# A four-layer graph network on one core: how layer 2's masks are applied, when they are made, and the order of TensorE's work

## The chip, the core and the metric

The kernel runs on one core of a Trainium2 chip. The core has five engines that matter here. TensorE (PE) multiplies matrices, with the loading of its stationary operand shown apart (PEld). VectorE (DVE) does elementwise work and reductions, ScalarE (ACT) functions of one argument and copies, GpSimd (POOL) a few powers. SyncE (SP) issues the transfers. Every engine works through its own queue in order and waits on semaphores for the others. The metric is the device time of one execution, in microseconds; less is better.

## The reference, cut to what matters

There are 32 graphs of 512 nodes with 256 features, and an adjacency matrix of 512 x 512 for each. Four attention layers follow each other, each with a residual and a layer norm around it:

```python
x = _layernorm(x + L0(x, adj))   # 4 heads; scores from two vectors, masked by adj, softmax, sum
x = _layernorm(x + L1(x, adj))   # 1 head, the same kind, elu
x = _layernorm(x + L2(x, adj))   # a transformer block, 8 heads, feed forward of 1024
x = _layernorm(x + L3(x, adj))   # 1 head, the same kind as layer 1
```

Layer 2 is the one that the change is about:

```python
allowed = (adj > 0) | (swapaxes(adj, 1, 2) > 0) | eye
scores = einsum('bhqd,bhkd->bhqk', q * scale, k)
scores = where(allowed[:, None], scores, -inf)
attn = softmax(scores, axis=-1)
ctx = einsum('bhqk,bhkd->bhqd', attn, v)
```

Layers 0, 1 and 3 use adj itself; layer 2 uses its symmetric closure with the diagonal.

## The kernel before

**Tiling.** A graph's 512 nodes lie in R = 4 blocks of 128 rows; the features in K = 2 blocks of 128. Each layer is written as a Python generator that yields ahead of each unit of TensorE's work. A unit is one block of rows of a projection, one block of columns of a transpose, one pair of score tiles, or one weighted sum.

**The order.** `graph(b)` (L711) strings the stages of graph b together, and `paced` (L101) gives every unit a key: `PERIOD * b` plus a number from the table `PLACES` (L31). `heapq.merge` (L729) runs the units of all graphs in the order of the keys. So work of three to four graphs is interleaved, and TensorE's order is exactly the order in which the units run (`manual_schedule` for that engine, L728). The order on the other engines is chosen by the scheduler of the language, and is fixed in the built program. Keys are only an order: they are no times.

**Stages and buffers.** The stages have buffer pools of their own: "a" for edges, layers 0 and 1, "b" for qkv, attention and projection, "c" for feed forward and layer 3. `bank` (L240) gives a PSUM bank: four for stage b, two each for a and c. `part` (L245) gives a tile of 128 x 512 from 8, 6 and 5 buffers. `project` (L311) makes a projection, with one buffer h in each stage.

**Edges and masks.** `load` (L340) loads adj transposed (adjt) and adj in two halves each, all four through one buffer. `masks` (L350) makes, on ScalarE, two passes over each half of adjt: a Copy into the byte mask `at` (3 buffers) and a Square, whose sums are compared later to verify that the entries are 0 or 1. Then VectorE takes the maximum with adj and with the identity on the diagonal. The first half becomes a byte mask a2m; the second half becomes a2a in bf16, turned into 0 or -2^127 (L370). All this stands at one place, `"edges"`, ahead of layer 0.

**Layers 0, 1, 3.** `along` (L328) lays a vector of a head along the free dimension with a transpose (gp) and a copy (gb). `kept` (L373) makes a tile of unnormalised attention in one VectorE step (L376): a maximum, times `at`. TensorE multiplies these tiles with the values (o; L403 in layer 0, L433 in layers 1 and 3). Layer 0 ends with a norm by head (`head_layernorm`, L275, with a power on GpSimd) and a layer norm (`layernorm`, L252, with another).

**Layer 2.** `qkv` (L468) makes q and k as sums of two parts (hi, lo), which 64 transfers a graph lay out in the tiles qk, and v. `attention` (L518) runs over four pairs of heads and four blocks j of keys. For each it makes two score tiles s (L527) and takes exp on ScalarE (L536). The mask comes in two ways: for j = 0 and 1 VectorE multiplies the exponentials of both heads with the byte mask (L539); for j = 2 and 3 TensorE adds 0 or -2^127 to the scores in PSUM, by a product of the identity with a2a (L535):

```python
if j in ADDED:
    nc.tensor.matmul(s, identb, a2[1][:, j % 2, :], start=False, stop=True)
nc.scalar.activation(t[:, i, :], s, AF.Exp, scale=QSCALE)
...
if j not in ADDED:
    edges = a2[0][:, j, :].unsqueeze(1).to_broadcast([P, 2, N])
    nc.vector.tensor_mul(t, t, edges)
```

Four such j are summed with v on TensorE (cp, L547) and copied (cs, L555). `attended` (L559) transposes cs, divides (L570, L574; ctx), transposes again (ctp) and projects (wop). `feed_forward` (L598) follows, with f1p, ft and f2p, and a residual and two norms; then `layer3` (L643).

**The engines' queues at these places.** SP issues the edge loads, x and xt, the qk layouts and the outputs, in one order. ScalarE's queue holds the Copy and Square passes between exps and evacuations; VectorE's holds the maxima between multiplications and norms.

## Time and profile before

| what | value |
|---|---|
| time, median of 3 runs (lowest, highest) | 3973.95 us (3971.76, 3975.07) |
| the profiled execution: its time, its span | 3970.98 us, 3969.2 us |
| granted TensorE clock, mean | 0.981 |
| L535, mask products on TensorE (385 of 512 on record) | 150.8 us busy, 392 ns listed |
| L539, multiplications by the mask on VectorE, x256 | 309.8 us busy, 1221 ns each |
| L536, exp on ScalarE, x1024 | 546.3 us busy, 605 ns listed |
| L361 and L364, Copy and Square passes | 1057 and 1041 to 1058 ns each |
| L366, maxima with adj | 1214 to 1216 ns each |
| ScalarE's wait at L361 for the load of adjt | 106.9 us, 32 times |
| ScalarE's wait at L361 for the mask buffer (DVE pt) | 20.0 us, 29 times |

How to read it: a row of the profile gives engine and line, operation, what it writes and reads, how often, and busy time with the mean of one. Consecutive instructions of one engine overlap at their ends, so the distance between two starts is the cost, and the listed duration is more than that. A wait names the instruction that ended it. Some records of products are missing from the trace.

### The profile page before, as it was taken

What the parts mean: (1) busy time and instruction counts of PE and PEld (TensorE: products, weight loads), DVE (VectorE), ACT (ScalarE), POOL (GpSimd) and SP (SyncE); (2) the same over time, 40 slices, a digit from 0 to 9 for tenths busy, and PEclk for the clock granted to TensorE, in tenths of its full rate; (3) what the DMA queues carried; (4) which work ended last, traced back from release to release, by engine and by line L of the source; (5) the groups of instructions that cost most, each with busy time, mean ns of one, the idle gap of its engine ahead of it and who ended that gap; (6) DMA issues with size and microseconds to landing.
All of it is one profiled execution on the core that took longest, in us unless ns stands there. A gap on an engine that the chain in (4) does not pass through costs nothing.

```text
span 3969.2 us, 53826 instructions
## 1 busy us (share of the span) xinstructions
PE 3806.5 (96%) x19367; PEld 2824.3 (71%) x19494; DVE 2523.9 (64%) x5402; ACT 1959.5 (49%) x4257; POOL 294.5 (7%) x266
## 2 busy tenths in 40 slices
PE   5899999999999999999999999999999999999996
PEld 4577767777767777777777777777777777777654
DVE  4557666667666667666667666667666667666543
ACT  2435555545555545555545555545455544555442
POOL 0000010000000000000000000000000000000000
PEclk6899999999999999999999999999999999999998
DMA  3222222222222222122222122222222222221110
GB/s 126 63 68 67 66 60 59 70 80 69 65 63 56 70 80 78 56 65 58 65 80 80 55 65 57 64 80 80 58 65 55 69 75 80 60 66 51 48 48 12
DMA packets 180432, 261.23 MB, mean 66 GB/s; under 512 B 36800, under 2 KB 72768, under 8 KB 180160
## 3 DMA queue, kind: packets, MB, share of 16 engines
q1 hardware_dynamic: 180160, 257.71, 23.3%
q8 instruction: 157, 2.57, 0.3%
q14 instruction: 115, 0.94, 0.1%
HBM read 106.57 MB, written 16.78 MB: 31 GB/s over the span
## 4 chain that ended last, share of the span: by engine, by line
PE 50%; DVE 17%; ACT 12%; issue 9%; POOL 5%; POOLq 0%; DVEq 0%; ACTq 0%
PE o L403 10%; ACT y L267 6%; PE f2p L627 6%; PE f1p L612 6%; PE o L433 6%; PE qkp L477 5%; POOL rs L262 3%; PE cp L547 3%; DVE pr L539 3%; PE h1p L318 3%; PE vp L504 3%; PE wop L588 3%; DVE bn L258 2%; POOL st L289 2%; PE gp L333 2%
## 5 line engine op out<-in xcount | busy, mean ns | idle before, releaser
L376 DVE SCALAR_TENSOR_TENSOR pt<-gb,ex,at 128x512 f32<-128x512 f32 x768 | 532.0, 745 | 359.2 <-ACT gb L337 358.4
L536 ACT ACTIVATE pr<-s 128x512 f32<-128x512 f32 x1024 | 546.3, 605 | 160.2 <-PE s L527 93.3
L267 ACT ACTIVATE y<-y,rs 128x256 f32<-128x256 f32 x768 | 398.5, 590 | 323.1 <-DVE rs L263 322.9
L403 PEld LDWEIGHTS o<-hv,pt 128*128 128x128 f32 x4096 | 506.4, 199 | 34.4 <-issue 20.2
L403 PE MATMUL o<-hv,pt 128*128 128x65 f32 x4096 | 503.3, 280 | 8.1 <-DVE pt L376 8.1
L433 PE MATMUL o<-h,pt 128*128 128x257 f32 x2048 | 488.2, 386 | 17.7 <-ACT exp L460 14.7
L627 PE MATMUL f2p<-wf,ft 128*128 128x256 f32 x2048 | 491.3, 383 | 10.6 <-ACT ft L621 5.3
L612 PE MATMUL f1p<-yt,wf 128*128 128x256 f32 x2048 | 488.7, 381 | 2.6 <-ACT yt L296 2.6
L547 PE MATMUL cp<-pr,v 128*64 128x512 f32 x2048 | 469.6, 600 | 3.7 <-DVE pr L539 3.7
L539 DVE TENSOR_TENSOR pr<-pr,a2m 128x1024 f32<-128x1024 f32 x256 | 309.8, 1221 | 253.2 <-ACT pr L536 253.1
L433 PEld LDWEIGHTS o<-h,pt 128*128 128x128 f32 x2048 | 375.7, 190 | 122.5 <-ACT exp L460 27.1
L527 PE MATMUL s<-qk 128*128 128x512 f32 x1024 | 450.4, 519 | 3.0 <-DMA qk<-lo 1.7
L627 PEld LDWEIGHTS f2p<-wf,ft 128*128 128x128 f32 x2048 | 379.2, 190 | 100.0 <-ACT ft L621 26.3
L612 PEld LDWEIGHTS f1p<-yt,wf 128*128 128x128 f32 x2048 | 384.7, 190 | 55.3 <-ACT yt L296 2.8
L621 ACT ACTIVATE ft<-f1p,cols 128x256 f32<-128x256 f32 x512 | 214.8, 471 | 401.6 <-PE f1p L612 401.6
L262 POOL TENSOR_TENSOR rs<-rs,mhalf 128x4 f32<-128x4 f32 x192 | 194.5, 1013 | 1904.7 <-DVE rs L261 1831.2
L547 PEld LDWEIGHTS cp<-pr,v 128*64 128x64 f32 x2048 | 136.0, 137 | 259.7 <-issue 229.5
L258 DVE BATCH_NORM_STATS2 bn<-y 128x6 f32<-128x256 f32 x768 | 297.3, 406 | 3.5
L337 ACT COPY gb<-gp 128x512 f32<-128x512 f32 x192 | 112.6, 586 | 338.3 <-PE gp L333 262.5
L477 PE MATMUL qkp<-xt,wqkv 128*128 128x512 f32 x512 | 236.5, 606 | 2.8 <-ACT xt L296 2.8
L527 PEld LDWEIGHTS s<-qk 128*128 128x128 f32 x1024 | 190.9, 194 | 57.9 <-issue 28.3
L411 DVE RECIPROCAL rd<-o 128x4 f32<-128x4 f32 x128 | 23.1, 181 | 270.9 <-PE o L403 270.9
(136 smaller groups left out, 4623.7 us busy)
## 6 DMA issues: line engine op xcount, KB each, us to landing
qk<-hi SPq DMA_DIRECT2D x1024, 64.0 KB, 2.0
qk<-lo SPq DMA_DIRECT2D x1024, 64.0 KB, 2.0
adjt<-in_adjt SPq DMA_DIRECT2D x64, 512.0 KB, 3.6
adj<-in_adj SPq DMA_DIRECT2D x64, 512.0 KB, 3.3
xt<-in_xt SPq DMA_DIRECT2D x32, 512.0 KB, 3.4
x<-in_x SPq DMA_DIRECT2D x32, 512.0 KB, 4.7
out<-y SPq DMA_DIRECT2D x32, 512.0 KB, 3.1
wf<-in_w1t SPq DMA_DIRECT2D x1, 1024.0 KB, 8.4
```

Of the source, the lines that this page charges most:

```text
L258: nc.vector.bn_stats(st[:, r, :], y[:, r, :])
L267: nc.scalar.activation(y[:, r, :], y[:, r, :], AF.Identity, bias=rs[:, 2, r : r + 1], scale=rs[:, 1, r : r + 1],)
L376: nc.vector.scalar_tensor_tensor(t, g, f, edges, op0=ALU.max, op1=ALU.mult)
L403: nc.tensor.matmul(o[:, r, :], pt[j][:, r * P : (r + 1) * P], hv[:, j, hh, :], start=j == 0, stop=j == R - 1,)
L433: nc.tensor.matmul(p[:, : D + 1], pt[j][:, r * P : (r + 1) * P], h[:, j, : D + 1], start=j == 0, stop=j == R - 1,)
L477: nc.tensor.matmul(p, wqkv[:, k, (s * K + c) * P : (s * K + c + 1) * P], xt[:, k, :], start=k == 0, stop=k == K - 1,)
L527: nc.tensor.matmul(s, qk[hp][:, 1, i, j * P : (j + 1) * P], qk[hp][:, 0, i, :], start=True, stop=j not in ADDED,)
L536: nc.scalar.activation(t[:, i, :], s, AF.Exp, scale=QSCALE)
L539: nc.vector.tensor_mul(t, t, edges)
L547: nc.tensor.matmul(cp[i * 2 * DH : (i + 1) * 2 * DH, :], v[:, j, first : first + 2 * DH], pr[j][:, i, :], start=j == 0, stop=j == R - 1,)
L612: nc.tensor.matmul(p[:, f, :], wf1[:, k, (ff + f) * P : (ff + f + 1) * P], yt[:, k, r * P : (r + 2) * P], start=k == 0, stop=k == K - 1,)
L627: nc.tensor.matmul(acc[:, i, :], ft[:, f, i * P : (i + 1) * P], wf2[:, ff + f, :], start=ff + f == 0 and i == 0, stop=ff + f == NF - 1 and ...
```

## The change

- `ADDED` and `SHUT` are gone: all 16 pairs of score tiles of a graph are multiplied by VectorE, and there is one byte mask a2 for all of adj's closure.
- The work on edges is split. `mask(b)` loads adjt half by half and makes `at` (now 4 buffers); the Square passes write into a `part` tile. `symmetric(b, at)` loads adj half by half and makes a2 (one buffer) in a stage of its own, `"mask"`, ahead of qkv.
- The first instruction of each such piece (the Copy, the maximum) is made to depend on the TensorE product that was issued last at its place (`product` records it, `in_place` adds the dependency). All products of the fast path are issued through `product`.
- `project` has two buffers h in stage a; `part` has seven in stage a for eight.
- Graph 0 loads xt and x ahead of its edges; xt's load stands ahead of the weights.
- All keys in `PLACES` are new.

```diff
-ADDED = (2, 3)
-SHUT = -(2.0**127)
 PERIOD = 1205
 PLACES = {
-    "edges": [-490],
-    "x": [-197],
+    "edges": [-226, -113, -5, -1],
+    "x": [84],
+    "mask": [1464, 1488, 1689, 1689],
     "layer 0": [
-        2, 11, 56, 83, 172, 302, 302, 302, 302, 302, 405, 405, 405, 405, 435, 533, 545, 545, 545,
-        553, 586, 586, 674, 674,
+        188, 232, 373, 373, 427, 532, 536, 536, 536, 549, 603, 603, 603, 630, 637, 712, 712, 728,
+        758, 758, 766, 779, 787, 791,
     ],
...
+    latest = [None]
+
+    def product(what, *args, **kwargs):
+        latest[0] = what(*args, **kwargs).ins.name
+
+    def in_place(op):
+
+        if latest[0]:
+            tc.add_manual_dep(op.ins, latest[0], ALL, reason="in its place")
+
...
-        return buf([P, N], "part", name, {"a": 8, "b": 6, "c": 5}[stage[0]])
+        return buf([P, N], "part", name, {"a": 7, "b": 6, "c": 5}[stage[0]])
...
-        h = buf([P, R, cols], "h", name, 1)
+        h = buf([P, R, cols], "h", name, {"a": 2}.get(stage[0], 1))
...
+    def half(b, name, h):
+        t = sb.tile([P, R // 2, N], I32, tag="adj", name=name, bufs=1)
+        rows = a[name][b, h * N // 2 : (h + 1) * N // 2]
+        nc.sync.dma_start(t, rows.rearrange("(r p) j -> p r j", p=P))
+        return t
+
+    def mask(b):
+
+        at = sb.tile([P, R, N], U8, tag="at", name="at", bufs=4)
         for h in range(2):
+            yield
+            t = half(b, "adjt", h)
             i = 2 * b + h
-            nc.scalar.activation(
-                at[:, half[h], :], adjt[h], AF.Copy, accum_out=sums[:, 0, i : i + 1]
-            )
-            nc.scalar.activation(a2[h], adjt[h], AF.Square, accum_out=sums[:, 1, i : i + 1])
+            yield
+            in_place(
+                nc.scalar.activation(
+                    at[:, h * R // 2 : (h + 1) * R // 2, :],
+                    t,
+                    AF.Copy,
+                    accum_out=sums[:, 0, i : i + 1],
+                )
+            )
+            squares = part("squares").bitcast(BF16).rearrange("p (r n) -> p r n", n=N)
+            nc.scalar.activation(squares, t, AF.Square, accum_out=sums[:, 1, i : i + 1])
+        return at
+
+    def symmetric(b, at):
+
+        a2 = sb.tile([P, R, N], U8, tag="a2", name="a2", bufs=1)
         for h in range(2):
-            nc.vector.tensor_max(a2[h], at[:, half[h], :], adj[h])
-        for r in range(R):
-            diag = a2[r * 2 // R][:, r % 2, r * P : (r + 1) * P]
-            nc.vector.tensor_max(diag, diag, identb)
-        nc.vector.tensor_scalar(a2[1], a2[1], 0.0, SHUT, op0=ALU.is_equal, op1=ALU.mult)
-        return at, a2
+            yield
+            t = half(b, "adj", h)
+            rows = slice(h * R // 2, (h + 1) * R // 2)
+            yield
+            in_place(nc.vector.tensor_max(a2[:, rows, :], at[:, rows, :], t))
+            for r in range(R // 2):
+                own = h * R // 2 + r
+                diag = a2[:, own, own * P : (own + 1) * P]
+                nc.vector.tensor_max(diag, diag, identb)
+        return a2
...
-                        stop=j not in ADDED,
+                        stop=True,
                     )
-                    if j in ADDED:
-                        nc.tensor.matmul(s, identb, a2[1][:, j % 2, :], start=False, stop=True)
                     nc.scalar.activation(t[:, i, :], s, AF.Exp, scale=QSCALE)
-                if j not in ADDED:
-                    edges = a2[0][:, j, :].unsqueeze(1).to_broadcast([P, 2, N])
-                    nc.vector.tensor_mul(t, t, edges)
+                edges = a2[:, j, :].unsqueeze(1).to_broadcast([P, 2, N])
+                nc.vector.tensor_mul(t, t, edges)
...
     def load_x(b):
         xt = sb.tile([P, K, N], F32, tag="xt0", name="xt0", bufs=1)
         nc.sync.dma_start(xt, a["xt"][b].rearrange("(k p) n -> p k n", p=P))
+        if b == 0:
+            weights0()
+        yield
         x = sb.tile([P, R, D], F32, tag="x", name="x")
         nc.sync.dma_start(x, a["x"][b].rearrange("(r p) d -> p r d", p=P))
-        yield
         return xt, x
...
-        at, a2 = yield from paced(b, "edges", load_all(b))
-        xt, x = yield from paced(b, "x", load_x(b))
+        if b == 0:
+            xt, x = yield from paced(b, "x", load_x(b))
+        at = yield from paced(b, "edges", mask(b))
+        if b:
+            xt, x = yield from paced(b, "x", load_x(b))
         x = yield from paced(b, "layer 0", layer0_all(b, x, xt, at, rds[0]))
         x = yield from paced(b, "layer 1", layer1_all(b, x, at, rds[1]))
+        a2 = yield from paced(b, "mask", symmetric(b, at))
         qk = yield from paced(b, "qkv", qkv_all(b, x))
```

What the new keys change in TensorE's order, read from the built programs: after the last layer-0 product of a graph the steps up to its layer-1 transposes are, in the new order, a feed-forward product f1p, two value projections, the scores of the first two pairs of heads of the graph before, with f2p, f1p, f2p, cp, f1p, f2p and cp between them. From the last f2p of the feed forward to layer 3's transposes come, in the old order, four score tiles with their masks, a layer-1 product, cp, three layer-1 products and the first steps of the next layer 0; in the new order two layer-1 products with two score tiles between them, cp, two more layer-1 products, and the transposes of the context and two layer-0 projections.

## The prediction

> **What bounds the kernel now.** I read the page's busy shares first, then the windows, to keep the ramps apart from the steady part, then the timeline of TensorE over some graphs, and last VectorE's timeline where attention runs. Busy shares and one wide window:

> ```profile
> span 3969.2 us, 53826 instructions
> PE 3806.5 (96%) x19367; PEld 2824.3 (71%) x19494; DVE 2523.9 (64%) x5402; ACT 1959.5 (49%) x4257; POOL 294.5 (7%) x266
> ...
> 200.00:3750.00 3550.00, 3491.87 (x18061) 2601.12 (x18181) 2336.50 (x5001) 1819.41 (x3959) 270.62 (x238) 1.00 0.24 67
> ```

> The window's columns are length, then busy time of TensorE, its weight loads, VectorE, ScalarE and GpSimd. TensorE works 98.4% of the middle. The other 105 us of its idle time lie in the first 200 and the last 220 us. The timeline shows one period, start of a graph's first layer-0 product to the next graph's:

> ```profile
> 1742.61 1.16 PE L318 MATMUL h0p<-w,xt 128*128 128x264 f32 x4 [0.34 <-ACT exp L460]
> 1861.21 1.16 PE L318 MATMUL h0p<-w,xt 128*128 128x264 f32 x4 [0.33 <-ACT exp L460]
> 1979.81 1.38 PE L318 MATMUL h0p<-w,xt 128*128 128x264 f32 x5 [0.34 <-ACT exp L460]
> ```

> The period is 118.60 us, the same each time: TensorE's order is fixed, and this is the sum of its steps and of a few waits that recur. What the mask costs there, and what a multiplication costs VectorE:

> ```profile
> 1803.60 1.04 PE L527 MATMUL s<-qk 128*128 128x512 f32 x2
> 1805.77 3.65 PE L547 MATMUL cp<-pr,v 128*64 128x512 f32 x16
> 1809.35 1.29 PE L527 MATMUL s<-qk 128*128 128x512 f32 x4
> 1810.48 1.89 PE L612 MATMUL f1p<-yt,wf 128*128 128x256 f32 x8
> ...
> 1813.23 1.23 DVE L290 TENSOR_TENSOR y<-y,st 128x1024 f32<-128x1024 f32 x1 [3.02 <-POOL st L289]
> 1814.37 1.22 DVE L539 TENSOR_TENSOR pr<-pr,a2m 128x1024 f32<-128x1024 f32 x1
> 1815.51 1.22 DVE L423 TENSOR_TENSOR y<-y,gam_b 128x1024 f32<-128x1024 f32 x1
> 1816.64 1.22 DVE L539 TENSOR_TENSOR pr<-pr,a2m 128x1024 f32<-128x1024 f32 x1
> ```

> Four scores with four added masks take 2.17 us (1803.60 to 1805.77), four without take 1.13 (1809.35 to 1810.48): a mask product costs 0.26 us of TensorE, whatever its listed 0.39. A multiplication costs VectorE 1.14 us, the distance between starts. VectorE also stands still for 3 us behind GpSimd's power (L289).

> [...]

> **The change, part by part.** Sums are per graph in the steady part, 118.60 us, and then over some 30 graphs, as the first and the last attention lie partly where TensorE idles anyway.

> *Removed.* 16 mask products of 0.26: 4.2 us of TensorE. On VectorE the L370 step, 0.4. The recurring stalls of the old order go too. In the period around 1861 TensorE's timeline shows 0.48 and 0.33 (layer 1's products and h0p, both behind ScalarE's exp L460) and 0.21 and 0.70 (h3p and gp, behind ScalarE). By strides it is more: three h3p projections take 3.96 us to the next gp (1867.99 to 1871.95) where three of 0.88 need 2.64, so 1.3 with the last two waits among it; layer 1's last three products take 0.9 too long, with the 0.48 among it; h0p 0.4 and some score pairs 0.4. I count 3.0. A stall-free period of the new order is then 118.6 - 4.2 - 3.0 = 111.4. Adding the new order's strides one by one gives 111.5.

> *Added to VectorE.* 8 multiplications a graph, 9.1 us: 256 x 1.14 = 292 us in all, less 13, so 2803 us or 71% of the span. On average that fits. It is the place that matters, so I walked one period of the changed order, engine by engine, with the durations of this trace (0.22 us from a product's end to its reader, 0.49 per exp in a row, 0.57 per copy of a bank, POOL 2.9 and 1.0). Three stretches:

> (a) From a graph's last layer-0 product to its layer-1 transposes TensorE has 23.2 us of steps, and the first two head pairs of the graph before fall there. VectorE must do layer 0's two norms (12 us), eight multiplications instead of four (9.1) and a feed-forward sum: 22 of 23.2. In the old kernel the stretch is 23.7 us with VectorE busy for 16.6. In the new order the fourth multiplication of the first head pair stands behind the step that waits for GpSimd's 2.9 us power; the weighted sum cp comes 0.4 late for it. ScalarE's Square of the next graph's edges (1.06 + 0.2) stands ahead of a feed-forward evacuation: 0.9. The second cp waits twice about 0.4 for its third and fourth multiplication, and the transposes 0.2 for ScalarE's normalisation. Together 2.0.

> (b) From there to layer 3: the sum that ends the feed forward now stands behind two multiplications and its norm behind a third, so that norm's end slips from 14.5 us after the last f2p product to about 17, while TensorE's steps up to layer 3's transposes shrink from 17.6 to about 15.4. On VectorE the context steps (L570, L574 of before) come after it. Layer 0's second projection waits 0.6 and the context's transposes 2.4 for these; layer 3's own transposes then find their data. Together 3.1.

> (c) The rest: 0.1 at gp, 0.45 for the fourth layer-0 tile of the third head. Together 0.6.

> So 111.5 + 5.7 = 117.2, against 118.6: 1.4 us less per graph, 42 us over 30.

> *Edges.* The Copy and Square passes on ScalarE (1.06 and 1.05 us) and the maxima on VectorE (1.21) remain the same in number. That each half has its own place ends ScalarE's waits of 106.9 us for adjt (3.3 a graph, its queue shut meanwhile) and 20.0 for the old mask buffer; TensorE hardly saw them, so nothing is booked. The ties to TensorE's order: the Copy waits for a product which by my walk is done a microsecond before; queued behind it are layer 1's copies and the next exps. The maximum waits for the context's transposes, 0.2 before VectorE comes to it; behind it are the copies of ct. I book 0; if they bind, 0.3 to 0.5 each. One buffer for layer 2's masks: the new first maximum comes 14 us of plan after the last multiplication of the graph before, so 0. SP's queue: 64 qk transfers a graph at 0.61 us are 39 us; the edge loads are put ahead of them and only block SP while nothing is due, so 0; if one slipped behind 16 of them, 10 us of ScalarE, which is not what the order shows.

> *Buffers.* Two h buffers: layer 1's products are over before the next layer 0 starts, so 0. Seven part buffers for eight: a head's four tiles are made after the previous head's products, so four are alive; 0, at worst one tile late (0.7 x 4 heads).

> *Start.* xt is loaded first, where the first product now waits until 10.71 us for it; VectorE's weights are ready at 7.8. Between 0 and -3, I take -3. Late maxima also leave graph 0's norm alone: within that.

> Sum: 3970.98 (the profiled run; its span is 3969.2) - 42 - 3 = 3926. The median of before is 3 us higher, so I say 3928.

> **Rivals.**
> 1. Mine, partly eaten saving: 3885 to 3965. For it: the walk. Against: it is one walk, and its 5.7 us of stalls have to be right to 1.4.
> 2. VectorE hides everything, as its 71% would suggest: stalls stay at 3.0, so -4.2 x 30 = -126: about 3848. Against: stretch (a) has no room.
> 3. Slower: VectorE's single queue becomes the bound in stretches (a) and (b), every multiplication delaying the norm and every norm delaying the next cp. Exposed, the 8 multiplications cost up to 9.1 us a graph; the saving decides against 4.2. From stalls of 7.2 us a graph on (1.5 above my walk) the change loses. I price it at stalls of 9: 111.5 + 9 = 120.5, +1.9 x 30 = +57: about 4030; all exposed would be +4.9 x 30, 4120.
> 4. No change that can be measured (within 0.2%, 8 us): the new stalls equal the saving: 3974. A change of order can hit this only by chance.

> **How the numbers follow.** Rival 1 has 0.52, rival 2 0.08, rival 3 0.32, rival 4 0.08. Walks leave waits out more easily than they invent them, hence 0.32. Faster is 0.60, same 0.08, slower 0.32; 0.2% is about what can be told from no change. The range leaves out most of rival 2 and the upper half of rival 3: 3870 to 4020. My own case alone: 3885 to 3965.

> **What would show it.** Right: a period near 117.2; the rows of L535 gone; the multiplication's row at 512 and about 1.2 us each; DVE busy near 2800; TensorE's waits led by the context's transposes behind ctx on VectorE, by cp behind pr, and by f2p behind ft; no wait of ScalarE for adjt. Wrong: a period under 115 (rival 2) or over 119 with cp, xt1p and xt3p waiting several microseconds for VectorE or its norms (rival 3), or a load of edges that ScalarE waits for.

## The result and the profile after

| what | before | after |
|---|---|---|
| time, median of 6 runs (lowest, highest) | 3974.01 us (3971.76, 3975.07) | 3958.30 us (3955.84, 3959.87) |
| ratio, 95% interval | | 0.9961 (0.9948 to 0.9973) |
| the profiled execution, its span | 3970.98, 3969.2 us | 3958.95, 3957.2 us |
| granted TensorE clock, mean | 0.981 | 0.973 |

The change gains 15.7 us, 0.4%. The forecast was 3928, a gain of 46. The top of the page after, then groups for two steps that the prediction priced, the multiplication by the mask (L551) and GpSimd's power in layer 0 (L296):

```profile
span 3957.2 us, 53344 instructions
PE 3722.2 (94%) x18982; PEld 2832.6 (72%) x18982; DVE 2830.4 (72%) x5626; ACT 1947.7 (49%) x4257; POOL 362.0 (9%) x266
...
L551 DVE TENSOR_TENSOR pr<-pr,a 128x1024 f32<-128x1024 f32 x512 | 616.7, 1216 | 220.4 <-ACT pr L549 220.2
...
L296 POOL TENSOR_TENSOR st<-st,mhalf 128x16 f32<-128x16 f32 x32 | 120.9, 3779 | 978.3 <-DVE st L295 978.3
```

VectorE is busy for 2830 us (forecast 2803), the multiplications are 512 of a listed 1.22 us each, where the forecast had added 1.14, the distance between starts. TensorE's busy time fell by 84 us, of which a 12 us gain is left in the profiled execution. The power takes 3.78 us on the mean; before it was 2.93.

All of TensorE's products go through one helper and have line L101 now, so they are told apart by their tiles. The waits after, as engine, tile, releaser, total us, times and longest (only those that the prediction spoke of):

```profile
PEld cp L101 <- DVE pr L551: 150.3, 128, 3.6
...
PE cp L101 <- DVE pr L551: 64.7, 65, 1.9
...
PE ctp L101 <- DVE ctx L586: 51.3, 61, 1.7
...
PE f2p L101 <- ACT ft L633: 22.9, 39, 3.2
...
PE h0p L101 <- DVE w L177: 11.6, 1, 11.6
...
ACT at L362 <- DMA adjt<-in_adjt: 11.5, 2, 11.3
```

A row that begins with PEld is the wait of the weight load for the same product. The three waits that the forecast named are there: cp behind the masked tiles, the context's transposes (ctp) behind ctx, f2p behind ft. ScalarE's wait for adjt fell from 106.9 to 11.5 us. At the start the first layer-0 product now waits 11.6 us for VectorE's weights instead of 10.71 for xt.

Now the period, in windows from a graph's first layer-0 product to the next graph's, and two windows of 3.4 us inside the first and the third. Columns: window, length, busy time of TensorE, weight loads, VectorE, ScalarE and GpSimd, granted clock, DMA share, GB/s.

```profile
1738.28:1857.17 118.89, 114.59 (x594) 87.84 (x593) 87.91 (x176) 60.71 (x133) 10.99 (x8) 0.99 0.24 67
1857.17:1976.07 118.90, 114.60 (x594) 87.66 (x593) 87.94 (x176) 60.79 (x133) 11.29 (x8) 0.99 0.24 67
1976.07:2093.28 117.21, 112.92 (x594) 86.45 (x593) 88.02 (x176) 60.69 (x133) 11.29 (x8) 1.00 0.24 68
1743.30:1746.70 3.40, 3.40 (x14) 2.99 (x13) 2.30 (x5) 2.26 (x5) 1.01 (x1) 0.50 0.28 60
1981.20:1984.60 3.40, 3.40 (x23) 3.04 (x22) 2.60 (x6) 3.11 (x7) 0.92 (x1) 1.00 0.31 93
```

Before, every period had 118.60 us. Now two of three have 118.9 and the third 117.21, which is the 117.2 of the forecast. In the long ones TensorE's granted clock is half for one stretch: the same place of the order takes 14 records there and 23 in the third period. The timeline of TensorE at this place, in the first of these periods and then in the third (start, us, tiles, number, idle time before it and what ended it):

```profile
1740.59 0.38 PE L101 MATMUL ctp<-ident,ctx 128*128 128x128 f32 x2
1741.23 0.33 PE L101 MATMUL ctp<-ident,ctx 128*128 128x128 f32 x1 [0.25 <-DVE ctx L586]
1743.00 1.13 PE L101 MATMUL ctp<-ident,ctx 128*128 128x128 f32 x5 [1.45 <-DVE ctx L586]
1743.93 1.06 PE L101 MATMUL xt3p<-ident,y 128*128 128x128 f32 x4
1744.78 2.88 PE L101 MATMUL h0p<-w,xt 128*128 128x264 f32 x8
...
1980.80 0.77 PE L101 MATMUL ctp<-ident,ctx 128*128 128x128 f32 x5 [1.45 <-DVE ctx L586]
1981.40 0.60 PE L101 MATMUL xt3p<-ident,y 128*128 128x128 f32 x4
1981.84 1.95 PE L101 MATMUL h0p<-w,xt 128*128 128x264 f32 x8
```

The wait for ctx is the same in both, 0.25 and 1.45 us. After it the eight layer-0 products take 2.88 us in the one period and 1.95 in the other, and the transposes are stretched too: 118.90 - 117.21 = 1.69 us a period. In the trace of the kernel after every halved stretch from 442 us to the end of the steady part lasts 3.41 us, and all of them begin on one grid of that step (from 678.30 to 3637.65 us are 867 steps of 3.413), of which the period is no multiple. The wait of 1.70 us in two pieces had such a stretch behind it in two periods of three. That it is two of three fits the grid: three periods are 355.0 us, 104 steps of 3.413, so the wait meets the grid in nearly the same way every third graph. (Only nearly: late in the run three periods in a row are long.)

From 442 us into the execution to the end of the steady part 19 such stretches lie in the trace: 19 x 1.69 = 32 us. In the trace of the kernel before none lies between 229 and 3765 us.

### The profile page after: what moved, and what is told of

Same layout as the page of the kernel before. It is cut to its first block, busy times and chain, and to the rows that moved or that the text cites. A ratio compares the mean times of both kernels' runs of the same rounds, so it can differ in the third digit from the quotient of the medians.

```text
span 3957.2 us, 53344 instructions
## 1 busy us (share of the span) xinstructions
PE 3722.2 (94%) x18982; PEld 2832.6 (72%) x18982; DVE 2830.4 (72%) x5626; ACT 1947.7 (49%) x4257; POOL 362.0 (9%) x266
## 4 chain that ended last, share of the span: by engine, by line
PE 51%; DVE 17%; issue 10%; ACT 7%; POOL 7%; SPq 2%; DMA 1%; DVEq 0%; POOLq 0%; ACTq 0%
PE o L101 12%; PE f1p L101 7%; PE f2p L101 6%; DVE pr L551 5%; PE cp L101 4%; POOL rs L269 4%; PE qkp L101 3%; PE h3p L101 3%; POOL st L296 3%; PE wop L101 3%; PE h1p L101 3%; ACT y L274 2%; SPq L510 2%; DVE bn L265 2%; ACT pr L549 2%
## 5 line engine op out<-in xcount | busy, mean ns | idle before, releaser
L551 DVE TENSOR_TENSOR pr<-pr,a 128x1024 f32<-128x1024 f32 x512 | 616.7, 1216 | 220.4 <-ACT pr L549 220.2
L101 PE MATMUL cp<-pr,v 128*64 128x512 f32 x2048 | 485.0, 605 | 64.7 <-DVE pr L551 64.7
L101 PEld LDWEIGHTS o<-hv,pt 128*128 128x128 f32 x4096 | 506.1, 198 | 32.6 <-DVE pt L391 16.0
L101 PE MATMUL o<-hv,pt 128*128 128x65 f32 x4096 | 507.2, 280 | 15.4 <-DVE pt L391 11.3
L101 PE MATMUL f2p<-wf,ft 128*128 128x256 f32 x2048 | 492.5, 383 | 23.2 <-ACT ft L633 22.9
L101 PE MATMUL f1p<-yt,wf 128*128 128x256 f32 x2048 | 488.7, 381 | 0.3 <-DVE yt L301 0.3
L101 PE MATMUL o<-h,pt 128*128 128x257 f32 x2048 | 482.5, 383 | 3.2 <-DVE pt L391 3.1
L101 PEld LDWEIGHTS o<-h,pt 128*128 128x128 f32 x2048 | 381.1, 190 | 97.0 <-ACT y L274 23.5
L101 PEld LDWEIGHTS f2p<-wf,ft 128*128 128x128 f32 x2048 | 379.1, 190 | 95.6 <-ACT ft L633 46.8
L269 POOL TENSOR_TENSOR rs<-rs,mhalf 128x4 f32<-128x4 f32 x192 | 234.9, 1224 | 2146.4 <-DVE rs L268 2092.5
L101 PEld LDWEIGHTS f1p<-yt,wf 128*128 128x128 f32 x2048 | 382.4, 190 | 52.3 <-issue 0.8
L101 PEld LDWEIGHTS cp<-pr,v 128*64 128x64 f32 x2048 | 127.9, 137 | 346.0 <-DVE pr L551 150.3
L101 PE MATMUL s<-qk 128*128 128x512 f32 x1024 | 359.1, 456 | 1.8 <-ACT pr L549 1.7
L101 PEld LDWEIGHTS s<-qk 128*128 128x128 f32 x1024 | 187.0, 190 | 97.9 <-issue 52.7
L101 PE MATMUL qkp<-xt,wqkv 128*128 128x512 f32 x512 | 232.2, 596 | 0.9 <-DVE xt L301 0.9
L296 POOL TENSOR_TENSOR st<-st,mhalf 128x16 f32<-128x16 f32 x32 | 120.9, 3779 | 978.3 <-DVE st L295 978.3
L567 ACT COPY cs<-cp 128x512 f32<-128x512 f32 x128 | 74.5, 582 | 259.6 <-PE cp L101 259.6
```

The source lines that it names most:

```text
L101: latest[0] = what(*args, **kwargs).ins.name
L269: nc.gpsimd.tensor_tensor(rs[:, 1, :], rs[:, 0, :], mhalf[:, :R], op=ALU.pow)
L296: nc.gpsimd.tensor_tensor(st[:, 2, :], st[:, 1, :], mhalf[:, :G], op=ALU.pow)
L567: nc.scalar.copy(t, cp)
```

## The experiments

All twelve at a glance. The period is the distance between the first layer-0 products of successive graphs, averaged over the 21 periods from the ninth graph to the thirtieth; the kernel after has 118.34.

| run | what differs from the kernel after | time, us | ratio to before (95%) | period, us |
|---|---|---|---|---|
| e1 | four fp32 products in the context's wait | 3999.63 | 1.0064 (1.0051, 1.0078) | 119.80 |
| e5 | sixteen short bf16 products there | 3923.33 | 0.9879 (0.9864, 0.9894) | 117.21 |
| e4 | the masks' part alone, in the kernel before | 4308.10 | 1.0842 (1.0828, 1.0857) | 129.70 |
| e6 | the new order, with the old masks | 4019.79 | 1.0121 (1.0106, 1.0137) | 120.55 |
| e2 | ctx ahead of layer 1's last two steps | 3938.48 | 0.9907 (0.9892, 0.9923) | 117.77 |
| e3 | e2, and the steps behind GpSimd issued later | 3902.34 | 0.9820 (0.9807, 0.9834) | 116.76 |
| e7 | ties around head pairs 0 and 1 | 3931.07 | 0.9904 (0.9889, 0.9919) | 117.82 |
| e8 | e7 and ties around the context | 3943.40 | 0.9927 (0.9914, 0.9941) | 118.04 |
| e9 | e3 and a mended context side | 3940.81 | 0.9913 (0.9899, 0.9927) | 117.95 |
| e10 | e9, fourth multiplication ahead, power spared | 3885.56 | 0.9776 (0.9762, 0.9789) | 116.04 |
| e12 | e10, layer 1's norm tied to a later place | 4026.25 | 1.0134 (1.0118, 1.0150) | 120.59 |
| e11 | after + e10's head-pair part + e5's filler | 3854.35 | 0.9704 (0.9691, 0.9717) | 114.87 |

### Is it the clock?

The theory: the forecast's walk was right, and the wait at ctp costs a second time through the clock. Rivals: the long h0p have another cause (banks, ScalarE's copies), or VectorE's load and GpSimd's longer power make the missing gain. To take the idleness away without the wait, TensorE gets products to do there that nobody reads:

```diff
             for r in range(R):
+                if name == "ct" and k == 0 and r == 2:
+                    for _ in range(4):
+                        product(nc.tensor.matmul,
+                            p[:, 2 * P :], ident, wo[:, 0, :], start=True, stop=True
+                        )
                 product(nc.tensor.transpose,
```

> The changed kernel with four more TensorE products per graph (ident by wo, 256 columns, about 0.44 us each, 1.76 us together; their result is overwritten), put between the second and the third of the context's transposes, where TensorE waits about 1.7 us for VectorE anyway. Theory 1 (this wait is what halves TensorE's granted clock for 3.41 us in two of three graphs, at 1.7 us each, 1.1 us a graph): the clock stays at 1.0 through the whole steady part, every period is about 117.2, and the time falls by 1.1 x 30 = 33 us to 3925. Theory 2 (the layer-0 projections behind that wait are long because their PSUM banks or ScalarE's copies are late): no halved clock is at fault, so nothing is gained, 3958 or up to 30 us more. Theory 3 (VectorE's load and GpSimd's longer power make the missing gain): no gain either; what of the 1.76 us doesn't fit into the wait comes on top, up to 53 us.

Measured: 3999.63 us, 41 slower than after. But the clock did what the theory says, 1.0 through all of the steady part (its mean over the whole span is 0.981, as in the kernel before; the kernel after has 0.973). The time was lost elsewhere. Two of TensorE's waits in this run, of which the kernel after has the first once and the second never:

```profile
PE h3p L101 <- DVE xt L301: 38.7, 29, 1.3
...
PE wop L101 <- ACT ct L303: 20.9, 29, 0.7
```

The orders on ScalarE and VectorE are made by the language's scheduler from its own estimate of times. Four fp32 products were enough to change them: the step of layer 1's norm that waits for GpSimd's power (L270) came ahead of the mask maximum on VectorE, its four scalings ahead of the copies of ct and xt3 on ScalarE, and the projections behind these wait. So this run changed two things and decides nothing on the sum. The next one has a filler so small that the orders of ScalarE, VectorE, GpSimd and SyncE are those of the kernel after, but for some dozen instructions in the first 350 us:

```diff
+                if name == "ct" and k == 0 and r == 2:
+                    for _ in range(16):
+                        product(nc.tensor.matmul,
+                            p[:, 2 * P : 3 * P], identb, identb, start=True, stop=True
+                        )
```

> The filler again, small enough that every engine's order in the steady part is that of the changed kernel (in the first filler run ScalarE's and VectorE's orders had moved with it): sixteen bfloat16 products of the identity by itself, 128 columns, in the columns of context row 2 ahead of its transpose, some 1 to 1.7 us in a wait of 1.7 us. Theory 1 (the wait halves the granted clock for 3.41 us in two of three graphs, and that costs 1.7 us each time): clock 1.0 all through, all periods about 117.2 instead of 118.9, 118.9, 117.2, time 3958 - 33 = 3925. Theory 2 (the halved clock only marks a longer period that has another cause): periods stay at a mean of 118.3 or grow, 3958 or more.

Measured: 3923.33 us. Three successive periods of this run:

```profile
1725.39:1842.61 117.22, 113.60 (x611) 87.41 (x609) 88.06 (x176) 60.64 (x133) 10.99 (x8) 1.00 0.24 68
1842.61:1959.82 117.21, 113.58 (x611) 87.40 (x610) 88.06 (x176) 60.64 (x133) 11.28 (x8) 1.00 0.24 68
1959.82:2077.03 117.21, 113.59 (x611) 87.39 (x609) 88.04 (x176) 60.65 (x133) 11.28 (x8) 1.00 0.24 68
```

Every period is 117.21, the clock 1.00. The group of context transposes takes as long as in the kernel after at full clock (3.01 us), and TensorE still waits 1.02 us in it. So the delay stayed, the half clock went, and 35 us with it (33 expected). With everything else in the same order, this shows the cause, and it leaves no room for the two rivals as an account of the missing gain: VectorE's load and GpSimd's power (3.81 us) are as in the kernel after.

### What the parts do alone

The masks' part by itself, in the order and with the buffers of before:

```diff
-ADDED = (2, 3)
+ADDED = ()
...
-        nc.vector.tensor_scalar(a2[1], a2[1], 0.0, SHUT, op0=ALU.is_equal, op1=ALU.mult)
...
-                    edges = a2[0][:, j, :].unsqueeze(1).to_broadcast([P, 2, N])
+                    edges = a2[j // 2][:, j % 2, :].unsqueeze(1).to_broadcast([P, 2, N])
```

> The kernel before with the masks' part of the change alone: all sixteen mask products leave TensorE and all sixteen multiplications are VectorE's, with the old order, the old places of the edge work and one projection buffer. If the forecast's sum for the masks (-4.2 us of products a graph, 8 x 1.2 us more on VectorE) holds in any order, TensorE's stalls grow by less than 4.2 and it lands near the changed kernel, 3900 to 3960. If the new order is what makes room on VectorE, the old order has the multiplications behind other VectorE work at cp: above 3974.

Measured: 4308.10 us, 334 slower than before. A period and the waits of this run:

```profile
1627.79:1757.48 129.69, 119.14 (x592) 89.02 (x592) 86.74 (x175) 60.94 (x133) 10.04 (x9) 0.96 0.22 62
```

```profile
PEld cp L546 <- DVE pr L538: 302.2, 165, 4.2
...
PE cp L546 <- DVE pr L538: 157.4, 100, 3.3
```

VectorE is busy for 86.7 of 129.7 us, so it isn't full, but cp waits up to 3.3 us for its multiplications, which stand behind other work. (h0p waits as well, 87.6 us in all, behind ScalarE's exp L459.) The clock is 0.96 over the period. If it is 1.0 or 0.5 as in the kernel after, that is some 10 us at half, about three stretches of 3.41 us, which at 1.69 us each (the kernel after's price) would be some 5 us; this is an estimate.

The other way round, the new order with the old masks:

```diff
-        a2 = sb.tile([P, R, N], U8, tag="a2", name="a2", bufs=1)
+        a2 = sb.tile([P, R // 2, N], U8, tag="a2", name="a2", bufs=1)
+        a2a = sb.tile([P, R // 2, N], BF16, tag="a2a", name="a2a", bufs=1)
...
-                        stop=True,
+                        stop=j < 2,
                     )
+                    if j >= 2:
+                        product(nc.tensor.matmul,
+                            s, identb, a2[1][:, j - 2, :], start=False, stop=True)
```

> The changed kernel, its order, its places and its buffers, with the masks as in the kernel before: for target groups 2 and 3 TensorE adds the mask, VectorE multiplies only for 0 and 1 (two small statistics tiles get one buffer instead of two, to make room). If the forecast's price of the mask products holds (16 x 0.26 = 4.2 us a graph) and the new waits at cp (2.4 us) and the halved clock (1.1) were VectorE's multiplications, the period is 118.3 + 4.2 - 3.5 = 119 to 120.5, and the time 3980 to 4025. If the new order is what gained and the masks' move costs more in waits than it saves, it is below 3958.

Measured: 4019.79 us and 120.55 us a period, at the upper end of what was expected, with the clock at 1.0 (0.982 in the mean). The new order with the old masks costs 1.95 us a graph against before, the new masks in the old order 11.1, and both together gain 0.3. So neither part gains by itself. That the new order is worth something because it makes room on VectorE where the multiplications fall fits these numbers, but no run shows it alone: the scheduler's orders differ in these two runs as well, and the numbers are those of whole kernels.

### Where the multiplications wait

Is the fourth multiplication late from load, or from what stands ahead of it in the queue? First the context. Layer 1's last two VectorE steps are issued behind the context multiplications:

```diff
+            if r:
+                yield
             nc.vector.scalar_tensor_tensor(y, m, 1.0, y, op0=ALU.min, op1=ALU.add)
```

> The changed kernel with layer 1's last two VectorE operations (L476 and L478, 0.64 and 0.68 us) issued behind the four context multiplications instead of ahead of the last two. The third and fourth context rows come 1.3 us earlier, so the 1.7 us wait of the context's transposes shrinks to about 0.4. Theory 1 (the wait halves the clock): without it no halved window is left, gain 1.3 + 1.1 = 2.4 us a graph, 3958 - 72 = 3886. Theory 2 or 3 (the clock is not the cause): only the wait's 1.3 us, 3919, and the layer-0 projections keep their 2.7 to 3.3 us. It could also give back what it gains where layer 1's output comes later (transposes xt2).

Measured: 3938.48 us, 52 more than theory 1 had. The wait at ctp fell by 0.8 us instead of 1.3, the clock stayed at 1.0 (0.982 in the mean), and the scheduler again put a step ahead of the copy of xt3: 1.1 us at h3p (31.2 us in 29 graphs), which the expectation had named only for another place. Then the same for head pairs 0 and 1:

```diff
         nc.gpsimd.tensor_tensor(st[:, 2, :], st[:, 1, :], mhalf[:, :G], op=ALU.pow)
+        yield
         nc.vector.tensor_mul(yg, yg, st[:, 2, :].unsqueeze(2).to_broadcast([P, G, HO]))
...
+        mv, rs = statistics(y, 1e-5)
+        yield
+        scaled(y, mv, rs)
```

> The same as the run before, and in layer 0 the two VectorE operations that wait for GpSimd's power (L297 and L270) issued later, behind the mask multiplications of head pairs 0 and 1, with layer 1's first transposes moved behind one feed-forward product group. If the fourth multiplication of head pairs 0 and 1 is late because it stands behind these two in VectorE's queue, the waits at cp (0.84 and 1.12 us) go: 1.9 us a graph more, 3886 - 58 = 3828 at best. If the fourth multiplication is late from load alone (VectorE busy without gaps there), the cp waits stay and the time is that of the run before.

Measured: 3902.34 us, 36 less than the run before, where up to 58 were expected. The second cp takes 3.85 us instead of 4.92: the queue theory holds there. The first stayed at 4.64, because a later place in the program doesn't bind the scheduler: it still put L297 ahead. So it was tied, as the change itself does with its edge work:

```diff
+        in_place(
             nc.vector.tensor_mul(yg, yg, st[:, 2, :].unsqueeze(2).to_broadcast([P, G, HO]))
+        )
```

> The changed kernel with three ties around head pairs 0 and 1: the multiplication that waits for GpSimd's power (L297) tied behind the feed-forward product after the pair's last scores, so that the fourth mask multiplication can't stand behind it; L270 issued behind pair 1's multiplications; the first Square tied into ScalarE's gap behind pair 1's exps, so that no ft evacuation stands behind it. Queue theory: the waits at f2p (0.85), at the first cp (1.06) and at the second cp (1.07) go, 3.0 us a graph, 3958 - 90 = 3868, with the halved clock still there. Load theory (VectorE simply has too much to do there): the cp waits stay or move to layer 1's transposes, 3920 to 3960.

> All of the run before, and the same for the context: layer 1's last two VectorE operations tied behind the second layer-0 projection, the first mask maximum later, layer 3's transposes together and its projections behind the second wop. If every wait of the changed kernel but the scheduler-independent ones (o0 0.3, gp 0.1, some 0.5) comes from what stands ahead in a queue, the period comes near 112 to 113 and the time to 3770 to 3800, with the clock at 1.0. If waits only move on, 3830 to 3900.

Measured: 3931.07 and 3943.40 us, 63 and at least 143 more than the queue theory had. In both the first cp fell to 3.58 us, no wait at all; but the second rose to 5.96 in most graphs. The half clock was still there in e7 (0.974 in the mean) and gone in e8 (0.982), as expected. The timelines of e8 at one such place, GpSimd's and then TensorE's:

```profile
1678.71 6.08 POOL L302 TENSOR_TENSOR st<-st,mhalf 128x16 f32<-128x16 f32 x1 [28.89 <-DVE st L301]
...
1692.87 3.49 PE L101 MATMUL cp<-pr,v 128*64 128x512 f32 x12 [1.47 <-DVE pr L574]
```

The power took 6.08 us. VectorE's timeline at the same place:

```profile
1678.54 1.22 DVE L574 TENSOR_TENSOR pr<-pr,a 128x1024 f32<-128x1024 f32 x1
1679.67 1.22 DVE L617 TENSOR_TENSOR y<-y,bo_b 128x1024 f32<-128x1024 f32 x1
1680.81 1.22 DVE L574 TENSOR_TENSOR pr<-pr,a 128x1024 f32<-128x1024 f32 x1
...
1684.82 1.23 DVE L305 TENSOR_TENSOR y<-y,st 128x1024 f32<-128x1024 f32 x1 [2.19 <-POOL st L302]
```

Three two-input steps (TENSOR_TENSOR with both inputs in SBUF) follow each other without a gap from just before the power's start to 1682.03; the power ends 2.76 us after that. In the kernel after one such step lies across the power's start and ends 1.05 us into it; the power takes 3.81, so it again ends 2.76 us later, and in one graph of the kernel before (at 157.18 us), where the step ends 1.15 us into it, it takes 3.91. In the other graphs there, with no such step at its start, it takes 2.90 to 2.92. So the fourth multiplication, and the addition of the output bias that the scheduler moved there with it, held up the very power that the next steps wait for: 6.08 us with the unbroken run of three, 3.81 with the one step. In 12 of 56 graphs of e7 and e8 (450 to 3700 us) the power took 3.8 with the same three steps; why then and not otherwise is open.

So, if the bias addition is kept away, the power should stay near 3.8. The context side was mended alongside, in a run of its own first:

```diff
-    "mask": [1464, 1488, 1689, 1689],
+    "mask": [1464, 1565, 1689, 1689],
...
-    "layer 3": [3958, 3998, 4038, 4074, 4074, 4074, 4082, 4179, 4182, 4185, 4185],
+    "layer 3": [3958, 3958, 4038, 4074, 4074, 4074, 4102, 4179, 4182, 4185, 4185],
```

> The third run's kernel (L297 and L270 issued later, no tie) with the context side mended: layer 1's last two VectorE operations tied behind the second layer-0 projection, the first mask maximum later, layer 3's transposes one after the other, its projections in their old place, its row of exponents one step later. In the run with all ties the context's waits went (1.37 to about 0.4 us) and came back as 2.6 us at layer 3's projections, whose copies stood behind the four scalings of layer 1's norm on ScalarE; here three of the four copies stand ahead of them. If that was the cause, the period falls from 116.8 to about 114.6, and the time from 3902 to 3836. If the wait comes back elsewhere, 3880 to 3905.

> The run before, with the fourth multiplication of pair 0 ahead of the one that waits for GpSimd's power, as in the two runs with ties, but with the output bias addition (1.2 us, two inputs) kept away from the power: about 2.9 us of VectorE's two-input work stand beside it instead of 4.2. If GpSimd's power is what VectorE's work lengthens (2.9 us with none beside it, 3.8 with 1.0, 6.1 with 4.2), it takes 3.8 to 5; near 3.8 the waits at f2p and the first cp (1.9 us) go without a new one at the second cp, and the time is 57 us under the run before, near 3780; at 6.1 the second cp waits 2 us and nothing is gained on the run before.

Measured: 3940.81 and 3885.56 us. The first is a miss of 105: layer 3's projections wait 2.1 us for ScalarE's copies (60.2 us in 29 graphs). In the steady part only one of the copies stood ahead of the four scalings, not three. And half clock followed this wait in about half of the periods (118.67 us where it did, 116.99 where it did not; the mean clock is 0.975). Two windows of the grid around the same wait of 2.06 us, the first followed by half clock, the second not:

```profile
1977.53:1980.94 3.41, 1.34 (x7) 0.85 (x6) 3.28 (x7) 2.73 (x7) 0.00 (x0) 1.00 0.22 86
2568.01:2571.42 3.41, 1.43 (x7) 1.26 (x8) 3.28 (x7) 2.46 (x7) 0.00 (x0) 1.00 0.12 43
```

In the first the whole wait lies inside, and TensorE is busy for 1.34 us of 3.41; the second begins after the wait has begun, and TensorE is busy for 1.43.

The second run gained 55.3 us on the first, with 57 expected (the 3780 itself fell with the first run's miss). Its timelines at the power, GpSimd's and VectorE's:

```profile
1660.04 3.80 POOL L302 TENSOR_TENSOR st<-st,mhalf 128x16 f32<-128x16 f32 x1 [28.89 <-DVE st L301]
...
1661.65 1.23 DVE L575 TENSOR_TENSOR pr<-pr,a 128x1024 f32<-128x1024 f32 x1 [0.56 <-ACT pr L573]
1662.79 0.68 DVE L676 TENSOR_TENSOR y<-f2p,y 128x512 f32<-128x512 f32 x1
1663.88 1.23 DVE L305 TENSOR_TENSOR y<-y,st 128x1024 f32<-128x1024 f32 x1 [0.41 <-POOL st L302]
```

VectorE now stands still for 0.56 us after the step that lies across the power's start; the power takes 3.80, though the fourth multiplication and another step run beside it later, at their usual lengths. The power ends 2.75 us after that step. So in these traces its length goes not with the amount of VectorE's work beside it, as the expectation had it, but with the unbroken run at its start. VectorE's wait for the power is 0.41 instead of 2.79 us in the kernel after, and both cp are near their stall-free 3.6 (3.58 and 3.90).

The wait at h3p was tried once more, by tying layer 1's norm behind layer 3's last projection:

```diff
+    def qkv(x, mv, rs):
+        scaled(x, mv, rs, in_place)
```

> The run with the power spared, with the wait of 2.06 us at layer 3's projections taken on: there ScalarE's four scalings of layer 1's norm, held by GpSimd's power, stand ahead of the copies of h3; here the operation that they wait for (L276 there) is tied behind layer 3's last projection, and layer 2's first transposes and layer 3's row of exponents come later. If that queue was the whole of the wait, the period falls from 116.0 to about 113.8 and the time from 3886 to 3820. If the norm is then late for layer 2's transposes, the gain is lost there: 3860 to 3890.

Measured: 4026.25 us, worse than both ranges. The wait at h3p is gone, but layer 2's transposes now wait for the norm (80.2 us, 112 times), and the clock is 0.952 in the mean. This was not followed further.

### Both cures together

```diff
+                    for _ in range(16):
+                        product(nc.tensor.matmul,
+                            p[:, 2 * P : 3 * P], identb, identb, start=True, stop=True
+                        )
...
+            if hp == 1 and b:
+                y = sb.tile([P, R, D], F32, tag="y2", name="y2", bufs=2)
+                in_place(nc.vector.tensor_add(y, x, all_rows(bo)))
...
+        in_place(
             nc.vector.tensor_mul(yg, yg, st[:, 2, :].unsqueeze(2).to_broadcast([P, G, HO]))
+        )
```

> The changed kernel with the cures that held so far and nothing else: the part of the run before that belongs to head pairs 0 and 1 (power spared, fourth multiplication ahead, first Square tied) and the small filler in the context's wait; VectorE's and ScalarE's orders around the context are those of the changed kernel. If the two cures are independent, the period is that of the filler run less what pairs 0 and 1 gained (0.39 at f2p, 1.06 at the first cp, 1.02 at the second): 117.21 - 2.47 = 114.74, and the time 3923 - 74 = 3849, with the clock at 1.0. If they are not (the context's wait takes up what comes earlier), 3885 to 3920.

Measured: 3854.35 us, against 3849 expected; the period is 114.87 against 114.74. One period of it:

```profile
1694.25:1809.13 114.88, 113.52 (x611) 87.50 (x610) 88.25 (x176) 60.51 (x133) 10.92 (x8) 1.00 0.25 69
```

The clock is 1.00, and the two cures add up. This kernel is 3.0% faster than before and 2.6% faster than after.

## Why the prediction was off, point by point

- **Direction right, size wrong.** 4.2 us of mask products go, and new waits behind VectorE's queue eat most of it. They arose where the walk had put them, but none of them had the size that it gave.
- **The period of the walk holds where the clock is full.** 117.2 forecast; 117.21 in every third graph and in every steady graph of e5. That it is so exact is luck in part, as the sizes below show. The whole sum, 3926 for the profiled execution, is 3922.44 in e5's.
- **The step that failed: 117.2 was taken for every graph.** The sum used durations at full clock, after the prediction had itself booked a wait of 2.4 us at the context's transposes and quoted a window with the clock at 1.00 from the kernel before, which has no such wait. With that wait, 1.70 us in the trace, the clock is 0.5 for 3.41 us in two of three graphs, 1.69 us each, 32 us in all; with the wait filled (e5) it is 1.00. The term "1.4 us less per graph, 42 us over 30" had to be 1.4 less 1.13, and came out at 118.60 - 118.34 = 0.26, 8 us. No rival named it.
- **Stretch (a), 2.0 us: too small.** In the third graphs f2p waits 0.85 us for ft (0.9 forecast), but the first cp is 1.06 late (0.4) and the second 1.34 (0.8 for two waits). Together about 3.2. The walk gave GpSimd's power 2.9 us; it takes 3.8 when a multiplication lies across its start.
- **Stretch (b), 3.1 us: too large.** 2.1 at the context's transposes (2.4), 0.1 at h0p (0.6): about 2.2.
- **Stretch (c), 0.6 us: too large.** 0.3, at the o0 tile. The three errors cancel by chance: 5.7 forecast, 5.7 found.
- **Start, -3 us: not seen where it was put.** The first product waits 11.6 us for VectorE's weights, where it waited 10.71 for xt: the forecast took the weights' 7.8 us from the kernel before, in which xt's load does not yet stand ahead of theirs. The graphs' first layer-0 products start 0.9 us later than before in the first graph, 2.0 earlier in the third and 7.9 earlier in the last; the other 4.1 of the 12 us lie behind that, in the last graphs' remaining work.
- **Edges and buffers at 0: nothing speaks against it.** The wait for adjt went and TensorE saw nothing of it. No run takes the ties or the buffers away alone.
- **Rival 3, at 0.32, was nearer than it looks.** e4 shows its waits, with the multiplications in the old order, where cp waits up to 3.3 us for them; but by the estimate above some 5 us a period of e4's loss is the half clock, which rival 3 did not name.

## What to carry to other kernels

Price a recurring wait of TensorE twice, for itself and for a stretch at half clock after it, if the trace of a kernel with such a wait shows one: here 1.70 us of waiting cost another 1.69 us in two graphs of three. Filling it with short products that nobody reads brought the second part back here (the period fell from 118.34 to 117.21 us), at no cost once the other engines' orders stayed as they were. Where a step waits for another engine, ask what stands behind it in the same queue, and what running that first does to the thing awaited.
